# A cross-attention, attention and expert kernel: q Wk^T formed turned, kept in SBUF and dealt by ScalarE and GpSimd; T tiles turned ahead; free expert places kept on chip

## The chip, the cores and the metric

The kernel runs on one core of one Trainium2 chip. The metric is device microseconds of one execution, as the median of several runs. The engines are TensorE (PE; PEld is its weight load), VectorE (DVE), ScalarE (ACT), GpSimd (POOL) and SyncE (SP, which only issues transfers). PSUM holds matmul results; GpSimd does not read it in this kernel.

## The reference

`x` is [8, 64, 512], the context is [8, 1601, 512], all fp32. Three residual steps follow each other.

```
# 1  cross-attention, one head of width 512
q = layernorm(x) @ Wq + bq;  k = ctx @ Wk + bk;  v = ctx @ Wv + bv
x = x + softmax(q @ k.T / sqrt(512)) @ v
# 2  self-attention over the 64 rows of a batch, 16 heads of 32
y = layernorm(x);  n = layernorm(y) * ln_w + ln_b
q, k = l2norm(n @ Wq), l2norm(n @ Wk);  v = y @ Wv
x = x + (sigmoid((q k^T - 0.29514) * 15) * (q.gq) * (k.gk)) @ v @ Wo + bo
# 3  one of 8 experts for each row
z = layernorm(x);  e = argmax(z @ gate_w.T);  zs = z * sigmoid(max logit)
x = x + (zs @ w_up[e].T * silu(zs @ w_gate[e].T)) @ w_down[e].T
```

## The kernel before

The 512 rows of x are four tiles of 128 rows; tile p holds batches 2p and 2p+1, so it is also called pair p. All matrix products are fp32.

**Cross-attention without keys.** Since q k^T = (q Wk^T) ctx^T + q.bk, the kernel never forms k. `project_q` (L278) makes `qpT`, the projected queries turned (columns on partitions). `keyed(p)` (L307) multiplies them by `wkT` into `qk`, 128 queries by 512 columns, with four products of 512 moving columns, and ScalarE copies that to a row tile. `biased` (L314) makes q.bk, which `unturned` (L329) brings into `qb`.

**Context and T tiles.** A pair's context is loaded by `load_group` (L205) in groups: g = 0, 1, 2 are slabs of 128 partitions by four chunks of rows, for each of the two batches (1 MB each), g = 3 is a tail of 65 rows. VectorE turns it in blocks of 32x32: `turn_group` (L230) fills one T tile, which is one quarter q of the 512 columns (four 32-column blocks) for one batch, in four steps, g = 0 to 3. A pair has eight T tiles of 416 keys. They come from a pool `blk` of five buffers; slabs come from a pool of twelve.

**R and the scores.** `scores` (L371) uses row groups: R holds for each 32-column block b the queries of that block, repeated on four groups of 32 partitions a, so that four products of 32 rows run beside each other, each on its own share of keys. For pair 0 R is filled by `spread` (GpSimd repeats the columns) and `fill_queries` (16 TensorE transposes, four ScalarE copies). For the other pairs `turn_queries` (L362) transposes `qk` with four TensorE transposes into PSUM, and `deal_queries` (L366) copies it into R on ScalarE with 16 copies of 32 partitions by 512. R has one buffer: the deals of pair p+1 start after the scores of pair p.

**After the scores.** `softmax` takes maxima on VectorE and four exponentials on ScalarE into `L`. `chances` (L417) transposes a block of `L` and copies it to `pt`; `attend` (L428) multiplies it with the context slabs. `at_turn`, `at_out` finish the tile (`p_po`), then `norm`, `turn`, `unit_q`, `unit_k`, `gates`, `values`, `split`, `align`, `sums`, `back`, `output` are the self-attention of the tile before it, spread between the steps of the pair that is running.

**Experts.** `gate` picks a row's expert (`oh` is its one-hot row). `route` (L733) finds the row's place among the rows of its expert: `pr` sums `ones` x the rows before (`runs`) and `before` x `oh`; `raised` (L773) lifts the count to the next part of 32 between tiles. GpSimd scatters the rows to DRAM (`xd`, `rd`); SP fetches them by part; `up_*`, `over`, `down` are the expert products.

**Order.** TensorE runs in the order of the program text throughout. ScalarE, VectorE and GpSimd do so inside `manual_schedule` blocks; elsewhere a planner orders them by modelled times. `keep_in_program_order` pins a single instruction. Idle transposes (`idle_turns`) stand at TensorE's start.

The main loop of pair p begins each quarter's scores like this, with the T tiles of the next quarter already asked for; the wait for the probabilities stands behind `p_po`:

```
if p == 1:
    keyed(NT - 1)
do((at_out, p - 1))
chance()
turned_qk = turn_queries(p + 1)
```

Of the kernel before, what the change touches and what calls it, by code (L numbers as in the profile page):

```python
# [36 lines left out]
def perceiver_kernel(ctx: ExitStack, tc: tile.TileContext, out: bass.AP, t: dict):  # L37
# [32 lines left out]
    xs = [const.tile([P, D], F32, tag=f"x{i}", name=f"x{i}") for i in range(NT)]  # L70

    def load_x(i):
        nc.sync.dma_start(out=xs[i], in_=t["x"][i * P : (i + 1) * P, :])
# [37 lines left out]
    bk, _ = load_c("xbk", [P, DC], nc.scalar)  # L111
# [93 lines left out]
    def load_group(p, g):  # L205
        got = []
        for b2 in range(2):
            src = t["ctx"][2 * p + b2]
            if g < 3:
                c = slab(f"cx_{p}_{g}_{b2}")  # L210
                rows = src[: 12 * P, :].rearrange("(q c) d -> q c d", c=12)
                nc.sync.dma_start(out=c, in_=rows[:, 4 * g : 4 * g + 4, :])
# [7 lines left out]
    for g in (3, 0, 1, 2):  # L220
        cxs[0, g] = load_group(0, g)
    
# [27 lines left out]

    order = ctx.enter_context(ExitStack())
# [4 lines left out]
    def normal(tiles):  # L256
        stats = []
        for i in tiles:
# [3 lines left out]
            stats.append((mean, rs))  # L262
        xns = []
        for i, (mean, rs) in zip(tiles, stats):
            nc.vector.reciprocal(rs, rs)
            xns.append(row(f"xn{i}"))
            nc.vector.tensor_scalar(xns[-1], xs[i], mean, rs, ALU.subtract, ALU.mult)
# [25 lines left out]
    idle_turns(14)  # L293
    first = {(q, b2): block_tile(0, q, b2) for q, b2 in ((0, 0), (0, 1), (1, 0), (1, 1), (2, 0))}
    with tc.manual_schedule(engines={mybir.EngineType.DVE, mybir.EngineType.Activation}):
        turn_x(0, normal([0])[0])
        project_q(0, 1, [bank(f"qp0_{ec}") for ec in range(DC)])
        later = normal(range(1, NT))
        for g in (3, 0, 1, 2):
            for b2 in range(2):  # L300
                for q in range(3):
                    if (q, b2) in first:
                        turn_group(first[q, b2], 0, q, b2, g)

    qks = {}

    def keyed(p, between=None):  # L307

        cols = slice(p * P, (p + 1) * P)
        ps = projected(qpT[:, :, cols], wkT, f"qk{p}", between)  # L310
        qks[p] = row(f"qk{p}")
        nc.scalar.copy(qks[p], ps)
# [21 lines left out]
    def spread(p):  # L334

        qk = qks.pop(p)
        got = []
        for b0 in range(0, NB, 4):
            q4 = rowp.tile([P, 4, 4, 32], F32, tag="row", name=f"q4_{p}_{b0}")
            nc.gpsimd.tensor_copy(  # L340
                q4,
                qk[:, 32 * b0 : 32 * b0 + 128].rearrange(
                    "p (b d) -> p b d", d=32
                ).unsqueeze(2).to_broadcast([P, 4, 4, 32]),
            )
            got.append(q4)
        return got

# [3 lines left out]

    def fill_queries(p, R, q4s, half):
        for b0 in range(8 * half, 8 * half + 8, 4):
            tp = bank4(f"rt_{p}_{b0}")
            for j in range(4):
                nc.tensor.transpose(
                    tp[:, j, :], q4s[b0 // 4][:, j, :, :].rearrange("p a d -> p (a d)"), ident
                )
            nc.scalar.copy(R[:, b0 : b0 + 4, :], tp)  # L360

    def turn_queries(p):  # L362

        return transposed(qks.pop(p), f"rt_{p}")

    def deal_queries(R, tp, a):  # L366

        for j in range(4):
# [882 lines left out]
```

## Time and profile before

| what | value |
|---|---|
| runs | 290.3, 293.19, 291.98 us; median 291.98 |
| the profiled execution | 290.53 us, of which the span from first to last instruction is 288.8 |
| TensorE busy | 277.4 us, 96% of the span |
| VectorE, ScalarE, GpSimd busy | 158.8, 114.8, 57.7 us |
| scores (L377) on TensorE | 1024 passes |
| T tiles (L232) on VectorE | 96 turns, 62.0 us, 682 ns each |
| R deals (L369) on ScalarE | 48 copies, 27.6 us, 576 ns each |
| moved by DMA | 57.70 MB, mean 200 GB/s |
| granted TensorE clock | 0.998 |

In the rows of a timeline the first number is the start in us from the span's start, the second the duration; then engine, line, operation, output<-inputs, shapes and the count of merged instructions; the bracket gives the idle time of that engine before the row and what ended it. In rows of groups the numbers behind the bar are busy us and mean ns of one. Matmuls are pipelined, so a row's duration is a little longer than the distance to the next row's start. A fp32 matmul of the program shows as two MATMUL rows; a transpose shows as one.

### The profile page before, as it was taken

The page shows a single profiled execution, that of the slowest core. Times are in us where ns is not written, and L with a number is a line of the kernel's source. Part 1 is how long each engine was busy: PE and PEld are TensorE (multiplying, and loading weights), DVE is VectorE, ACT ScalarE, POOL GpSimd, SP SyncE. Part 2 cuts the span into 40 slices and gives each one's busy share as a digit, 9 for nine tenths or more (in the row PEclk, how much of TensorE's full clock was granted, in tenths as well). Part 3 has the DMA queues.
Part 4 walks back from the last instruction along what each step waited for, and adds up shares of the span by engine and source line. Part 5 has one row for each costly group of instructions (what it writes and reads, how often), then busy time and mean ns, then how long its engine had stood idle before and what let it go on. Part 6 is the DMA issues. An engine that isn't in the chain of part 4 may idle for free. (4 is left out here: it accounts for less than half of the span.)

```text
span 288.8 us, 6414 instructions
## 1 busy us (share of the span) xinstructions
PE 277.4 (96%) x2625; PEld 136.8 (47%) x2625; DVE 158.8 (55%) x413; ACT 114.8 (40%) x240; POOL 57.7 (20%) x102
## 2 busy tenths in 40 slices
PE   6999999999999999999999999999999999999991
PEld 4856564436553345555334564443454455343320
DVE  2465487438532776956498694552371476374130
ACT  2232303782057483317769325631426334130110
POOL 5030524000631003100220400022060032413302
PEclk9999999999999999999999999999999999999999
DMA  6999594099799991000499003969990200533401
GB/s 189 350 398 403 188 338 184 3 355 419 268 297 369 406 412 27 5 3 0 161 391 375 22 2 98 341 195 357 376 378 9 75 0 2 161 93 128 168 1 44
DMA packets 20288, 57.70 MB, mean 200 GB/s; under 512 B 2274, under 2 KB 10514, under 8 KB 16544
## 3 DMA queue, kind: packets, MB, share of 16 engines
q1 hardware_dynamic: 17568, 50.37, 48.1%
q0 software_dynamic: 2400, 6.89, 6.7%
q8 instruction: 22, 0.36, 0.5%
q14 instruction: 10, 0.08, 0.1%
q10 hardware_dynamic: 288, 0.00, 0.1%
HBM read 50.94 MB, written 6.84 MB: 200 GB/s over the span
## 5 line engine op out<-in xcount | busy, mean ns | idle before, releaser
L232 DVE STREAM_TRANSPOSE T<-cx 128x512 f32<-128x512 f32 x96 | 62.0, 682 | 23.4 <-DMA cx<-in_ctx_dram 20.4
L377 PE MATMUL sc<-T,R 32*64 32x416 f32 (+2 forms) x1024 | 50.0, 501 | 0.5 <-DVE T L232 0.5
L433 PE MATMUL ac<-cx,pt 128*64 128x512 f32 x192 | 43.8, 598 | 0.0
L377 PEld LDWEIGHTS sc<-T,R 32*64 32x64 f32 x1024 | 26.7, 131 | 17.9 <-issue 5.7
L369 ACT COPY R<-t_rt 32x512 f32<-32x512 f32 x48 | 27.6, 576 | 0.8
L433 PEld LDWEIGHTS ac<-cx,pt 128*64 128x64 f32 x192 | 12.7, 136 | 22.1 <-issue 21.2
L1059 PE MATMUL gu<-wgu,xeT 128*32 128x512 f32 x192 | 22.9, 597 | 0.0
L509 POOL TENSOR_TENSOR gm_k<-qn_k,c_gk 128x512 f32<-128x512 f32 x4 | 5.1, 1271 | 62.7 <-DVE qn_k L504 62.7
L283 PE MATMUL qp<-xnT,w_xWq 128*128 128x128 f32 (+1 forms) x64 | 16.3, 426 | 0.5 <-ACT xnT L274 0.5
L472 POOL TENSOR_TENSOR x<-x,c_bo 128x512 f32<-128x512 f32 x4 | 5.1, 1269 | 55.6 <-DVE xh L471 55.6
L185 PE MATMUL p_q<-w_aWq,xhT 128*128 128x512 f32 x32 | 14.8, 605 | 0.1
L185 PE MATMUL p_qk<-w_xWkT,qpT 128*128 128x512 f32 x32 | 14.6, 598 | 0.1
L185 PE MATMUL p_k<-w_aWk,xhT 128*128 128x512 f32 x32 | 14.7, 596 | 0.0
L388 DVE TENSOR_REDUCE mx<-sc 128x1 f32<-128x416 f32 (+2 forms) x16 | 8.1, 567 | 11.9 <-PE sc L377 11.9
L185 PE MATMUL p_po<-w_xWv,acT 128*128 128x512 f32 x32 | 14.6, 592 | 0.0
L185 PE MATMUL p_o<-w_aWo,cT 128*128 128x512 f32 x32 | 14.5, 596 | 0.0
L185 PE MATMUL p_v<-w_aWv,xvT 128*128 128x512 f32 x32 | 14.4, 592 | 0.0
L283 PEld LDWEIGHTS qp<-xnT,w_xWq 128*128 128x128 f32 x64 | 11.7, 234 | 5.3 <-ACT xnT L274 0.9
L423 ACT COPY pt<-pp 128x512 f32<-128x512 f32 (+1 forms) x16 | 8.1, 505 | 12.8 <-PE pp L421 12.8
L1094 PE MATMUL y<-wd,hT 128*32 128x512 f32 x96 | 11.5, 596 | 0.3 <-ACT hT L1086 0.3
L399 ACT ACT_TABLE_LOAD x3 | 3.8, 1283 | 17.7 <-DVE bias L394 17.7
L1069 DVE TENSOR_TENSOR h<-gu,h 128x256 f32<-128x256 f32 x6 | 2.5, 425 | 14.1 <-ACT h L1068 14.1
(203 smaller groups left out, 377.5 us busy)
## 6 DMA issues: line engine op xcount, KB each, us to landing
cx<-in_ctx_dram SPq DMA_DIRECT2D x24, 1024.0 KB, 10.0
wgu<-in_wgT_dram SPq DMA_DIRECT2D x8, 512.0 KB, 9.2
wgu<-in_wuT_dram SPq DMA_DIRECT2D x8, 512.0 KB
wd<-in_wdT_dram SPq DMA_DIRECT2D x8, 512.0 KB, 7.3
rd<-blank POOLq DMA_DIRECT2D x6, 258.0 KB, 5.5
in<-rd SPq DMA_DIRECT2D x6, 258.0 KB, 3.8
xd<-blank POOLq DMA_DIRECT2D x6, 256.0 KB, 4.8
in<-xd SPq DMA_DIRECT2D x6, 256.0 KB, 7.2
```

The lines of the kernel that those rows point to most:

```text
L185: nc.tensor.matmul(ps, lhsT=srcT[:, dc, :], rhs=w[:, dc, :], start=(dc == 0), stop=(dc == DC - 1),)
L232: nc.vector.transpose(T[:, :, 128 * g : 128 * g + 128].rearrange("p b (c k) -> p b c k", k=32), cxs[p, g][b2][:, :, 128 * q : 128 * q + 12 ...
L283: nc.tensor.matmul(ps[ec][:, : n * P], lhsT=wq[:, dc, ec * P : (ec + 1) * P], rhs=xnT[:, dc, cols], start=(dc == 0), stop=(dc == DC - 1),)
L369: nc.scalar.copy(R[32 * a : 32 * a + 32, j::4, :], tp[32 * j : 32 * j + 32, :, :])
L377: nc.tensor.matmul(sc[a][r : r + S, : WIDTH[a]], lhsT=R[32 * a : 32 * a + 32, b, r : r + S], rhs=Ts[b2][32 * a : 32 * a + 32, j, : WIDTH[a ...
L388: nc.vector.tensor_reduce(mx[:, a : a + 1], sc[a][:, : WIDTH[a]], AX.X, ALU.max)
L423: nc.scalar.copy(pt[:m, :nch, :], tp[:m, :nch, :])
L433: nc.tensor.matmul(ac[r : r + S, :], lhsT=pt[:m, j, r : r + S], rhs=rhs, start=(g == 0 and j == 0), stop=(g == 3),)
L472: nc.gpsimd.tensor_tensor(xs[i], xs[i], bo, ALU.add)
L509: nc.gpsimd.tensor_tensor(heads(gm), heads(qn), gb.unsqueeze(1).to_broadcast([P, H, HD]), ALU.mult)
L1059: nc.tensor.matmul(ps[c, :], lhsT=xTs[k][:, dc, c], rhs=ffw[e][0][:, dc, :], start=(dc == 0), stop=(dc == DC - 1),)
L1094: nc.tensor.matmul(y[c, :], lhsT=hT[:, ic, c], rhs=ffw[e][1][:, ic, :], start=(ic == 0), stop=(ic == IC - 1),)
```

## The change

**q Wk^T turned.** `keyed` now takes `wkT` as the stationary operand and `qpT` as the moving one, so the result comes out with columns on partitions, for one pair (128 moving columns) or for two (256). `keep_keyed` copies it to SBUF (`qkTs`). `turn_queries`, `spread` and `fill_queries` are gone. `deal_queries` reads SBUF, for parts by ScalarE and for parts by GpSimd: for pair 0 two of four partition groups each, for pair 1 all on ScalarE, for pairs 2 and 3 half of each group. A group's deals stand in the turn of the same number.

**Opening.** x becomes one tile, loaded in two transfers; Wq in two instead of four. The tails of pair 0 and `bk` move from the SP and ScalarE queues to GpSimd's, behind a copy that reads the end of Wq. `later = normal(1..3)` stands before `project_q(0)`, and `normal` finishes each tile while the next one's root is taken. There are 15 idle turns and then 2 more. Seven T tiles of pair 0 are asked for at once (two of them in slabs) and turned in the order g = 0, 1, 3, then 2. The first quarter's scores run in two key ranges, 0 to 256 ahead of `biased`, 256 on after group 2 is turned. The whole of pair 0's scores stands inside the manual order.

**Main loop.** Pairs 1 and 2 call `at_out(p - 1, chance)`: the first probability block is transposed between the second and the third product of `p_po`.

**Free places.** `route` makes two products, `before` x `oh` and `ones` x `oh`; VectorE keeps the running counts (`free`) and lifts them to the next part; `raised` and the last product `pc` are gone.

```
-    load_x(0)
+    load_x(0, 1)
     wq = slab("w_xWq")
-    for dc in range(DC):
-        nc.sync.dma_start(out=wq[:, dc, :], in_=t["xWq"][:, dc, :])
-    for i in range(1, NT):
-        load_x(i)
+    for dc in (0, 2):
+        nc.sync.dma_start(out=wq[:, dc : dc + 2, :], in_=t["xWq"][:, dc : dc + 2, :])
+    load_x(1, NT - 1)
...
-    bk, _ = load_c("xbk", [P, DC], nc.scalar)
...
-                nc.sync.dma_start(out=c[: SK - 12 * P, :], in_=src[12 * P :, :])
+                queue = nc.gpsimd if p == 0 else nc.sync
+                ins = queue.dma_start(out=c[: SK - 12 * P, :], in_=src[12 * P :, :])
+                if p < 2:
+                    tc.keep_in_program_order(ins)
...
-    for g in (3, 0, 1, 2):
+    for g in (0, 1, 2):
         cxs[0, g] = load_group(0, g)
...
+    small_loads = tiny(1, "held", "small_loads")
+    tc.keep_in_program_order(nc.gpsimd.tensor_copy(small_loads, wq[:, DC - 1, 0:1]))
+    cxs[0, 3] = load_group(0, 3)
+    bk = load_late("xbk", [P, DC])
...
-    idle_turns(14)
+    idle_turns(15)
     first = {(q, b2): block_tile(0, q, b2) for q, b2 in ((0, 0), (0, 1), (1, 0), (1, 1), (2, 0))}
-    with tc.manual_schedule(engines={mybir.EngineType.DVE, mybir.EngineType.Activation}):
-        turn_x(0, normal([0])[0])
-        project_q(0, 1, [bank(f"qp0_{ec}") for ec in range(DC)])
-        later = normal(range(1, NT))
-        for g in (3, 0, 1, 2):
...
+    for q, b2 in ((2, 1), (3, 0)):
+        T = slabs.tile([P, DC, D], F32, tag="slab", name=f"T_0_{q}_{b2}")
+        first[q, b2] = T[:, :, :416]
...
+    begin = tc.manual_schedule(engines={mybir.EngineType.DVE, mybir.EngineType.Activation})
+    begin.__enter__()
+    turn_x(0, normal([0])[0])
+    later = normal(range(1, NT))
+    idle_turns(2)
+    project_q(0, 1, [bank(f"qp0_{ec}") for ec in range(DC)])
+    for g in (0, 1, 3):
+        turn_first(g)
...
-        ps = projected(qpT[:, :, cols], wkT, f"qk{p}", between)
-        qks[p] = row(f"qk{p}")
-        nc.scalar.copy(qks[p], ps)
...
+        for c in range(DC):
+            if c == DC // 2 and between is not None:
+                between()
+            for ec in range(DC):
+                nc.tensor.matmul(
+                    ps[c * n // DC][:, c % (DC // n), :, :],
+                    lhsT=wkT[:, ec, c * P : (c + 1) * P], rhs=qpT[:, ec, cols],
+                    start=(ec == 0), stop=(ec == DC - 1),
+                )
+        return ps
...
-    def deal_queries(R, tp, a):
...
-        for j in range(4):
-            nc.scalar.copy(R[32 * a : 32 * a + 32, j::4, :], tp[32 * j : 32 * j + 32, :, :])
+    def deal_queries(R, qkT, a, js=range(4), copy=nc.scalar.copy):
...
+        for j in js:
+            copy(R[32 * a : 32 * a + 32, j::4, :], qkT[32 * j : 32 * j + 32, :, :])
...
-        if i > 0:
-            nc.tensor.matmul(pr, lhsT=ones, rhs=runs[-1], start=True, stop=False)
-        nc.tensor.matmul(pr, lhsT=before, rhs=oh[:, i, :], start=(i == 0), stop=True)
...
+        nc.tensor.matmul(ps[:, :E], lhsT=before, rhs=oh[:, i, :], start=True, stop=True)
+        nc.tensor.matmul(ps[:, E : 2 * E], lhsT=ones, rhs=oh[:, i, :], start=True, stop=True)
+        at = tiny(E, "at", f"at{i}")
         if i > 0:
...
+            nc.vector.tensor_tensor(at, ps[:, :E], free[i - 1], ALU.add)
+            nc.vector.tensor_tensor(at, at, oh[:, i, :], ALU.mult)
...
-        for g in range(4):
+        for g in (0, 1, 3, 2):
             cxs[p, g] = load_group(p, g)
...
-    with tc.manual_schedule(engines={mybir.EngineType.Activation}):
-        def turn_later():
-            for i in range(1, NT):
-                turn_x(i, later[i - 1])
...
-        keyed(0, turn_later)
-    q4s = spread(0)
+    R = queries(0)
+    for i in range(1, NT - 1):
+        turn_x(i, later[i - 1])
+    keep_keyed(0, keyed(0, between=lambda: turn_x(NT - 1, later[-1])))
+    for a in range(2):
+        deal_queries(R, qkTs[0], a)
+        deal_queries(R, qkTs[0], 2 + a, copy=nc.gpsimd.tensor_copy)
     project_q(1, NT - 1, [bank(f"qp1_{ec}") for ec in range(DC)])
-    R = queries(0)
-    fill_queries(0, R, q4s, 0)
-    fill_queries(0, R, q4s, 1)
...
+    sc = [bank(f"sc_0_{a}") for a in range(4)]
+    scores(0, 0, R, sc, [first[0, 0], first[0, 1]], hi=256)
     qbT = biased()
...
+    turn_first(2, range(3))
+    turn_first(2, (3,))
+    scores(0, 0, R, sc, [first[0, 0], first[0, 1]], lo=256)
+    first[3, 1] = blocks(0, 3, 1)
+    for q in range(1, 4):
+        scores(0, q, R, sc, [first[q, 0], first[q, 1]])
+        if q == 1:
+            unturned(qbT)
+    begin.__exit__(None, None, None)
...
             if p == 1:
-                keyed(NT - 1)
-            do((at_out, p - 1))
-            chance()
-            turned_qk = turn_queries(p + 1)
+                qk = keyed(NT - 1)
+            at_out(p - 1, chance)
+            if p == 1:
+                keep_keyed(NT - 1, qk)
...
             if 0 < p < NT - 1 and g > 0:
-                deal_queries(R, turned_qk, g - 1)
+                deal_queries(R, qkTs[p + 1], g, range(2))
+                deal_queries(R, qkTs[p + 1], g, range(2, 4), nc.gpsimd.tensor_copy)
...
-    ps = bank("pc")
-    nc.tensor.matmul(ps[:, :E], lhsT=ones, rhs=runs[-1], start=True, stop=True)
```

More of the change, by code (lines that the diff above doesn't have):

```diff
@@ L261, in normal @@
             nc.scalar.activation(rs, var, AF.Sqrt, bias=eps)
[L262 to L267, printed above, removed]
+            if stats:
+                finish(i - 1)
+            stats[i] = mean, rs
+        finish(tiles[-1])
         return xns
@@ L332, in unturned, with scores @@
         nc.vector.tensor_copy(qb, tp[:, 0, ::32])
[L334 to L347, printed above, removed]
     def queries(p):
         return one.tile([P, NB, P], F32, tag="R", name=f"R_{p}")
[L353 to L371 removed]
+    def deal_queries(R, qkT, a, js=range(4), copy=nc.scalar.copy):
+        for j in js:
+            copy(R[32 * a : 32 * a + 32, j::4, :], qkT[32 * j : 32 * j + 32, :, :])
+    def scores(p, q, R, sc, Ts, js=range(4), lo=0, hi=D):
         for j in js:
@@ L694, in tables @@
         )
-    runs = []
+    free = []
     def gate_parts(i):
@@ L963, in perceiver_kernel @@
         if p == 0:
-            for k in range(1, NT):
-                if k < NT - 1:
-                    keyed(k)
-            tables()
+            qk = keyed(1, 2)
         else:
```

108 lines of the change are left out of this document (58 added, 50 removed).

## The prediction

> **What bounds the kernel now.** I read the page first, then the TensorE timeline from the start, then the waits and the timelines of the other engines around each step that moves.
>
> ```profile
> PE 277.4 (96%) x2625; PEld 136.8 (47%) x2625; DVE 158.8 (55%) x413; ACT 114.8 (40%) x240; POOL 57.7 (20%) x102
> ...
> PE   6999999999999999999999999999999999999991
> ```
>
> TensorE is busy 96% of the span of 288.8 us, in every slice but the first and the last. So a part of the change is worth what it takes off TensorE's queue, or what it adds there as waiting. The second view is the TensorE timeline of the opening (start us, duration us, line, tiles, xcount):
>
> ```profile
> 7.19 5.84 PE L283 MATMUL qp<-xnT,w_xWq 128*128 128x128 f32 x32 [0.46 <-ACT xnT L274]
> 13.17 1.95 PE L185 MATMUL p_qk<-w_xWkT,qpT 128*128 128x512 f32 x4
> ...
> 16.42 1.88 PE L185 MATMUL p_qk<-w_xWkT,qpT 128*128 128x512 f32 x4
> 18.14 10.48 PE L283 MATMUL qp<-xnT,w_xWq 128*128 128x384 f32 x32
> 28.46 1.91 PE L357 MATMUL rt<-ident,q 128*128 128x128 f32 x16
> ...
> 32.75 3.02 PE L377 MATMUL sc<-T,R 32*64 32x416 f32 x62 [0.54 <-DVE T L232]
> ```
>
> Each fp32 product is two passes. A pass of 512 columns takes 1.72/4 = 0.43 us (from 16.42 to 18.14), one of 384 takes 10.32/32 = 0.3225 us (18.14 to 28.46): 0.84 ns a column with next to nothing fixed, so 0.11 for 128 columns and 0.22 for 256. A transpose costs 1.84/16 = 0.115. The first projection is slower: asked for by windows, 18 of its 32 passes start between 7.19 and 11.19 (0.21 each), the other 14 take 1.84 us. TensorE's only wait for data here is the 0.54 us before 32.75. The scores of pair 0 end at 45.05. The third view is VectorE's timeline:
>
> ```profile
> 9.41 0.69 DVE L138 BATCH_NORM_STATS2 st_a<-x 128x6 f32<-128x512 f32 x1 [3.85 <-DMA x<-in_x_dram]
> ...
> 31.99 1.30 DVE L232 STREAM_TRANSPOSE T<-cx 128x512 f32<-128x512 f32 x2 [1.68 <-DMA cx<-in_ctx_dram]
> ```
>
> The first context slab of pair 0 is turned at 18.38, the sixth landed just before 31.99, and the first T tile after it (0.65 us) ends TensorE's 0.54 us wait.
>
> **The opening.** Removed there: 16 transposes `rt` (28.46 to 30.30, 1.84 us), the GpSimd `spread` and four ScalarE copies. `keyed(0)` becomes 32 passes of 128 columns, 32 x 0.11 = 3.57 us against 8 x 0.43 = 3.43: +0.14. The three extra idle transposes sit in TensorE's waits before 5.62 (0.35) and 7.19 (0.46) and cost nothing while those stand; without that cover, 3 x 0.23 (3.25/14 of the idle row) = 0.7.
>
> The moved step that matters is `later = normal(...)`: its three square roots now stand on ScalarE ahead of the four `qpT` activations of tile 0, and TensorE's `keyed(0)` is queued behind those. Call L the landing of the one transfer that now holds x1 to x3. From the rows of VectorE (0.69 + 0.18 for a tile's moments, 0.16 + 0.55 for its finish, 0.3 for a root) the third root ends at L + 3.7, `qpT` (1.14) at L + 4.8. Before, x1's moments start at 9.41 and the third tile's at 11.03 without waiting, so all three had landed by 11.03; fewer SP issues (0.46 us each) and half the small ScalarE loads are ahead of it now. I take L = 10.0, with bounds 9.3 and 11.0. Then `keyed(0)` starts at 14.7 instead of 13.17, but with two of the three x transposes behind it; 1.79 + 0.44 + 1.79 later, at 18.7, the 384-column projection starts (18.14 before), and it ends at 29.05.
>
> The first-range scores follow: 64 passes of 256 columns, 3.02 x 256/400 = 1.95, needing only slabs 0 and 1 (landed at 25.9, turned by 28), then `biased` 1.08, to 32.1. Here the second range needs slab 2: landing 31.99 as before, or earlier by up to 2 us because pair 1's tails no longer sit behind it on the same queue; plus 0.65. I take 32.3. The second range (144 columns in the mean, 1.1 to 1.7; I take 1.3), then three quarters (9.09) and `t_qb` (0.33) give 43.1: **-1.9**. With L = 9.3 and an early slab it is 42.1, -2.9; with L = 11.0 and 0.4 more for the split quarter 44.2, -0.8. The other T tiles follow on VectorE 0.65 us apart, ahead of the quarters that read them.
>
> Two more queues are touched. Pair 0's tails and `bk` move to GpSimd, behind a copy that waits for Wq: three issues of 0.53 to 0.75 us, where GpSimd had nothing to do from 4.5 to 18.98. A load from this queue landed 9.2 us after its issue (`c_lnw`), so about 19; the tails are turned at 28, `bk` is read at 31. And two T tiles take the slabs that the two `held` tiles had, so pair 1's second slab pair starts at about 39.5 and 43 instead of 32. A slab took 2.5 us behind another; VectorE asks for it at about 48, and TensorE for the result near 64. Both cost nothing.
>
> GpSimd's part here is eight copies of 32x512 from one set of partitions to another, between 19.4 and about 30. No row has that form. Bounds from the nearest:
>
> ```profile
> L509 POOL TENSOR_TENSOR gm_k<-qn_k,c_gk 128x512 f32<-128x512 f32 x4 | 5.1, 1271 | 62.7 <-DVE qn_k L504 62.7
> ...
> L340 POOL COPY q<-qk 128x512 f32<-128x512 f32 x4 | 2.3, 609 | 14.5 <-ACT qk L312 14.5
> ```
>
> 0.61 us (a copy of as many elements a partition) to 1.27 (two inputs). I take 0.61, the same operation: 4.9 us; at 1.27 it is 10.2, to 29.6, when the last block of the first quarter is just being reached. Hidden at both ends. [...]
>
> [...]
>
> **Later TensorE work.** The 12 transposes `t_rt` go (134.74 to 135.18: 0.44 for four): -1.31. The paired `keyed(1, 2)` is 32 x 0.218 = 6.95 against 6.87, `keyed(3)` as above: +0.08 + 0.14. Routing has 8 small products instead of 10 at 0.22: -0.44; VectorE's extra 8-column adds (0.17) hide behind the 8 us between the last `pr` and the transposes that need its rows.
>
> **A new wait.** In tiles 1 and 2 the first probability block (`pp`) moves from behind `p_po` to its middle.
>
> ```profile
> 126.94 0.66 PE L177 MATMUL t_at<-ident,acs 128*128 128x128 f32 x4
> 127.43 3.60 PE L185 MATMUL p_o<-w_aWo,cT 128*128 128x512 f32 x8
> 130.87 3.60 PE L185 MATMUL p_po<-w_xWv,acT 128*128 128x512 f32 x8
> 134.30 0.60 PE L421 MATMUL pp<-ident,L 128*128 128x128 f32 x4
> 134.74 0.60 PE L177 MATMUL t_rt<-ident,qk 128*128 128x128 f32 x4
> ```
>
> ```profile
> 129.82 1.28 ACT L399 ACT_TABLE_LOAD   x1 [1.54 <-DVE bias L394]
> ...
> 132.85 0.58 ACT L399 ACTIVATE L<-sc,bias 128x384 f32<-128x384 f32 x1
> ```
>
> In tile 2 the scores end at 126.94; `t_at` 0.49, `p_o` 3.44 and half of `p_po` 1.71 bring TensorE to `pp` at 132.58. The fourth exponential ends at 133.43, the one-column one at 133.67: ScalarE loaded its table only after the bias came. TensorE stands 1.05 us, with the second half of `p_po`, the x transposes and all of `attend` queued behind it. If the table is loaded early, the wait is 0. I take 1.05, since this stage's own rows are the nearest. In tile 1 the new `pp` falls at 83.9, after the exponentials' end at 83.66: no wait.
>
> **A wait that shrinks.** ScalarE made 16 deals (0.576 each) per pair; in pairs 2 and 3 it now makes 8, so `sq_k` no longer sits behind four of them (2.37 us from 106.36), nor does the chain over GpSimd's `gm_k` to `kT`, for which TensorE stands 0.58 us before 118.40 and 0.34 before 167.99. VectorE's order may eat part of it: between 0 and -0.92, I take -0.7. GpSimd's deals for pair 3 queue behind the row scatter that ends at 150.1; four at 0.61 end at 152.5, the scores start at 160.65.
>
> **Sum.** -1.9 - 1.31 + 0.22 - 0.44 + 1.05 - 0.7 = **-3.1 us**. The profiled execution took 290.53 (span 288.8), so 287.4; its median of runs is 291.98, 1.45 above it, and I predict **288.9** on that level. All good ends together (-2.9, no wait, -0.92) give -5.4, or 286.6; all bad ends (-0.8, +1.05, 0) -1.3, or 290.7. Runs of one kernel spread about 1 us around their median.
>
> **Rivals.** (1) *The full gain*: the table of tile 2 loads early, the slab lands early: -4.2 to -5.4, about 287.2. For it: pair 1's tails, two transfers of 65 rows, run beside the last slab, and the rate falls there; against it: the table load in the row above stood behind its wait. (2) *The opening gives nothing back*: transfers set the end of pair 0's scores and the x chain comes late: 291.98 - 1.3 to -1.9, about 290.4. For it: six waits of VectorE for slabs, 6.9 us, up to 36 us; against it: the first range now covers what TensorE would wait. (3) *GpSimd's deals become the bound*, and it is slower: place, the first quarter's scores; eight deals of c each have about 11.2 us (19.4 to 30.6) before its last block, so from c = 1.4 us it costs, and from (11.2 + 3.1)/8 = 1.8 the whole gain is gone. At 2.4 us, four times the row, it costs 8: 296.9. Against it: `gs`, a GpSimd copy across partitions, costs 186 ns for 8 elements, the same as a straight one-column copy.
>
> **Chances.** Forecast 0.46, (1) 0.22, (2) 0.22, (3) 0.06, other slower orders 0.04. A measurement of this kernel can tell about 1%, 2.9 us. The forecast's own spread lies a little more than half beyond that, so faster 0.5, within 1% 0.38, slower 0.12 (with part of (2)). The likeliest case alone spans 288.0 to 289.9; the range for 8 in 10 is 285.6 to 291.8.
>
> **What would show it.** Right: no `rt` or `t_rt` rows; scores of pair 0 ending near 43; a TensorE wait of about 1 us on ScalarE's `L` in tile 2; GpSimd deals near 0.6 us; no wait of scores on GpSimd. Wrong: a deal over 1.4 us, `keyed(0)` starting after 16, scores of pair 0 ending after 44.5, or `keyed` passes of 128 columns over 0.13 us, which would add 0.02 x 64 or more.

## The result and the profile after

The changed kernel took 303.53 us in the median of four runs, the kernel before 291.46 on the same chip: a ratio of 1.041, 95% interval 1.036 to 1.047. It is 12 us slower. The forecast was 288.9, in a range up to 291.8. (The 291.98 given ahead of the prediction is the median of three of the four runs of before.)

The profiled execution took 303.54 us, with a span of 301.8 against 288.8. The page of the changed kernel, first TensorE's share and instruction counts, then its busy tenths and its granted clock in 40 slices of the span:

```profile
PE 276.7 (92%) x2724; PEld 142.4 (47%) x2724; DVE 159.6 (53%) x420; ACT 110.1 (36%) x230; POOL 70.8 (23%) x120
...
PE   7699989999999339999899999999999999999991
...
PEclk9989999999999859999999999999999999999997
```

TensorE's busy time is lower than before (276.7 against 277.4), so the work did shrink. But two slices show 3 where before had 9 throughout, and the clock row dips in the same slices, and once near the start. The starts of the same steps in the three timelines of TensorE say where the time went. (The third column is an experiment described below: the blank rows put first.)

| TensorE reaches | before | after | blank rows first |
|---|---|---|---|
| end of pair 0's scores | 44.97 | 46.04 | 46.05 |
| first `p_q` (tile 0) | 100.32 | 110.48 | 102.25 |
| first `al` | 118.40 | 129.36 | 119.57 |
| `t_at` after pair 2's scores | 126.94 | 138.38 | 128.07 |
| pair 2's attention `ac` | 136.14 | 148.20 | 137.89 |
| first `t_xe` (expert rows) | 214.03 | 226.81 | 215.64 |
| end of the span | 288.8 | 301.8 | 290.7 |

Of 13.0 us, 1.07 arise in the opening and 9.1 more by the first `p_q`. Another 0.8 come by the first `al` and 2.0 in all behind it. TensorE's timeline at that place (start, duration, in the bracket the idle time and what ended it):

```profile
99.65 1.08 PE L451 MATMUL ac<-tail,pt 65*64 65x512 f32 x4
110.48 5.26 PE L185 MATMUL p_q<-w_aWq,xhT 128*128 128x512 f32 x8 [9.75 <-DVE xhT L498]
```

TensorE stands 9.75 us for `xhT`, the scaled turned rows of tile 0. Then its `p_q` takes 5.26 us instead of 3.70. The same row of before has no wait:

```profile
100.32 3.70 PE L185 MATMUL p_q<-w_aWq,xhT 128*128 128x512 f32 x8
```

VectorE makes half of `xhT`; its timeline after, and then the two waits for slabs that stood in the same place before:

```profile
100.99 1.30 DVE L237 STREAM_TRANSPOSE T<-cx 128x512 f32<-128x512 f32 x2 [7.00 <-DMA cx<-in_ctx_dram]
...
107.85 0.71 DVE L237 STREAM_TRANSPOSE T<-cx 128x512 f32<-128x512 f32 x1 [5.37 <-DMA rd<-blank]
...
110.06 0.37 DVE L498 TENSOR_SCALAR xhT<-t_xh,c_lnw,c_lnb 128x128 f32<-128x128 f32 x1
```

```profile
93.83 0.71 DVE L232 STREAM_TRANSPOSE T<-cx 128x512 f32<-128x512 f32 x1 [3.56 <-DMA cx<-in_ctx_dram]
...
96.32 1.31 DVE L232 STREAM_TRANSPOSE T<-cx 128x512 f32<-128x512 f32 x2 [1.59 <-DMA cx<-in_ctx_dram]
```

`xhT` is queued on VectorE behind T tiles of pair 2. One of these waited 7.00 us for a context slab, a later one 5.37 us for a transfer `rd<-blank`. That T tile takes one of the five `blk` buffers, the one in which `blank` lies: a zero tile that `blank_rows` (L667) writes twelve times to the expert rows in DRAM. GpSimd's timeline after, and then its memset before, say why this is late:

```profile
79.39 1.91 POOL L385 COPY R<-qkT 32x512 f32<-32x512 f32 x3 [34.05 <-PE sc L395]
81.35 0.52 POOL L669 MEMSET blank<- 128x512 f32 x1
...
82.53 0.56 POOL L672 DMA_DIRECT2D xd<-blank  x1
...
91.03 0.54 POOL L673 DMA_DIRECT2D rd<-blank  x1 [3.69 <-DMA rd<-blank]
93.17 0.54 POOL L672 DMA_DIRECT2D xd<-blank  x1 [1.60 <-DMA xd<-blank]
95.47 0.54 POOL L673 DMA_DIRECT2D rd<-blank  x1 [1.76 <-DMA rd<-blank]
```

```profile
74.78 0.53 POOL L651 MEMSET blank<- 128x512 f32 x1 [28.05 <-PE sc L377]
```

Three deals of pair 2 stand in GpSimd's queue ahead of the `blank` memset. The planner put them there; in the text `blank_rows` comes first. A deal writes R, and R is free only when pair 1's scores end, at 79. So the memset ran at 81.35 instead of 74.78. The twelve transfers then began just as SP started pair 2's slabs (83.70). From issue to landing they took, in the answers for that tile, first after and then before:

```profile
DMA to landing us min/median/max: 2.5/11.5/14.9
```

```profile
DMA to landing us min/median/max: 4.2/5.2/7.7
```

The last one is issued at 95.47, against 82.42 before, as GpSimd waits three times for its own earlier transfers.

In this trace the granted clock falls behind the waits. The same trace by stretches (from:to, length, busy time of TensorE, weight loads, VectorE, ScalarE, GpSimd, then the granted clock, the share of the DMA engines and GB/s):

```profile
7.84:14.66 6.82, 4.37 (x37) 3.97 (x37) 3.94 (x12) 1.55 (x7) 3.05 (x10) 1.00 1.04 403
14.66:18.08 3.42, 3.42 (x18) 3.42 (x17) 1.25 (x3) 1.32 (x4) 0.00 (x0) 0.50 1.02 328
...
103.41:113.65 10.24, 3.17 (x4) 1.51 (x5) 5.80 (x12) 2.62 (x5) 0.00 (x0) 0.50 1.00 418
```

The clock is full from 7.84, half from 14.66 to 18.08, full again, and half for 10.24 us after the long wait began. Before, it was full from 11.42 to 287.9 without a break. (7.84 and 11.42 are the starts of the trace's first clock records. The views count the time ahead of them as full, but TensorE is slow there: four transposes of x take 1.12 us at 5.61, against 0.60 at 18.32.)

The opening, in TensorE's timeline:

```profile
7.18 4.14 PE L299 MATMUL qp<-xnT,w_xWq 128*128 128x128 f32 x32
12.90 0.66 PE L177 MATMUL t_xn<-ident,xn 128*128 128x128 f32 x4 [1.57 <-DVE xn L274]
14.44 0.89 PE L177 MATMUL t_xn<-ident,xn 128*128 128x128 f32 x4 [0.88 <-DVE rs_a L272]
15.12 3.37 PE L343 MATMUL qk<-qpT,w_xWkT 128*128 128x128 f32 x16
...
18.75 1.95 PE L343 MATMUL qk<-qpT,w_xWkT 128*128 128x128 f32 x16
20.54 10.49 PE L299 MATMUL qp<-xnT,w_xWq 128*128 128x384 f32 x32
...
39.24 0.87 PE L395 MATMUL sc<-T,R 32*64 32x385 f32 x7 [1.25 <-issue]
...
46.04 1.13 PE L343 MATMUL qk<-qpT,w_xWkT 128*128 128x256 f32 x4
```

The first projection is faster (4.14 instead of 5.84 us). Then come two waits for x1 and x2 (1.57 and 0.88), the first half of the key products at half clock (3.37 us, the second half 1.95), and near 38 us a wait that ends with "issue", which means that it ends with nothing that the profile shows.

### The profile page after: what moved, and what is told of

It is laid out like the page before. It is cut to its first block, busy times and chain, and to the rows that moved or that the text cites. A ratio compares the mean times of both kernels' runs of the same rounds, so it can differ in the third digit from the quotient of the medians.

```text
span 301.8 us, 6627 instructions
## 1 busy us (share of the span) xinstructions
PE 276.7 (92%) x2724; PEld 142.4 (47%) x2724; DVE 159.6 (53%) x420; ACT 110.1 (36%) x230; POOL 70.8 (23%) x120
## 5 line engine op out<-in xcount | busy, mean ns | idle before, releaser
L395 PE MATMUL sc<-T,R 32*64 32x416 f32 (+5 forms) x1088 | 50.3, 482 | 1.2 <-issue 1.2
L385 POOL COPY R<-qkT 32x512 f32<-32x512 f32 x24 | 14.5, 604 | 56.1 <-PE sc L395 45.6
L185 PE MATMUL p_q<-w_aWq,xhT 128*128 128x512 f32 x32 | 16.4, 659 | 9.8 <-DVE xhT L498 9.8
L385 ACT COPY R<-qkT 32x512 f32<-32x512 f32 x40 | 24.6, 616 | 0.7
L343 PE MATMUL qk<-qpT,w_xWkT 128*128 128x128 f32 (+1 forms) x96 | 16.2, 332 | 0.0
L185 PEld LDWEIGHTS p_q<-w_aWq,xhT 128*128 128x128 f32 x32 | 6.4, 211 | 19.7 <-DVE xhT L498 12.3
L343 PEld LDWEIGHTS qk<-qpT,w_xWkT 128*128 128x128 f32 x96 | 14.9, 213 | 1.4 <-issue 0.7
L185 PE MATMUL p_k<-w_aWk,xhT 128*128 128x512 f32 x32 | 14.7, 596 | 0.0
L299 PE MATMUL qp<-xnT,w_xWq 128*128 128x128 f32 (+1 forms) x64 | 14.6, 388 | 0.0
L503 ACT ACTIVATE xhT<-t_xh,c_lnb,c_lnw 128x128 f32<-128x128 f32 x8 | 3.7, 458 | 25.7 <-DVE xhT L498 25.7
## 6 DMA issues: line engine op xcount, KB each, us to landing
rd<-blank POOLq DMA_DIRECT2D x6, 258.0 KB, 11.5
xd<-blank POOLq DMA_DIRECT2D x6, 256.0 KB, 11.6
```

Of the source, the lines that this page charges most:

```text
L185: nc.tensor.matmul(ps, lhsT=srcT[:, dc, :], rhs=w[:, dc, :], start=(dc == 0), stop=(dc == DC - 1),)
L299: nc.tensor.matmul(ps[ec][:, : n * P], lhsT=wq[:, dc, ec * P : (ec + 1) * P], rhs=xnT[:, dc, cols], start=(dc == 0), stop=(dc == DC - 1),)
L343: nc.tensor.matmul(ps[c * n // DC][:, c % (DC // n), :, :], lhsT=wkT[:, ec, c * P : (c + 1) * P], rhs=qpT[:, ec, cols], start=(ec == 0), s ...
L385: copy(R[32 * a : 32 * a + 32, j::4, :], qkT[32 * j : 32 * j + 32, :, :])
L395: nc.tensor.matmul(sc[a][r : r + S, lo : min(hi, WIDTH[a])], lhsT=R[32 * a : 32 * a + 32, b, r : r + S], rhs=Ts[b2][32 * a : 32 * a + 32, ...
```

## The experiments

The ratio is always to the kernel before, run beside each on the same chip, with its 95% interval. "Theory A" for the large loss is the chain just read: deals ahead of the blank rows, late writes that collide with the slabs, a buffer that stays taken, and `xhT` behind T tiles.

**Blank rows first.** The GpSimd deals of pair 2 are pinned behind what the text has in front of them. Only GpSimd's order differs.

```
+    behind = {
+        1: lambda to, of: tc.keep_in_program_order(nc.gpsimd.tensor_copy(to, of)),
+        2: nc.gpsimd.tensor_copy,
+    }
...
-                deal_queries(R, qkTs[p + 1], g, range(2, 4), nc.gpsimd.tensor_copy)
+                deal_queries(R, qkTs[p + 1], g, range(2, 4), behind[p])
```

> The kernel after, with GpSimd's eight query deals for pair 2 pinned behind the two memsets and twelve transfers of the blank rows; every other engine's order is as in after. Theory A (late blanks: the deals wait for scores(1) to end, so the blank rows are written 6.6 us later, run into pair 2's context loads and keep VectorE's next T tile waiting for their buffer): the blank transfers are issued from about 75 us as before, the 9.75 us wait of p_q for xhT falls below 1 us, the cold clock behind it goes too, and the time is 303.5 - 11 = 291.5 to 292.8. Rival B (pair 2's context is late because of its own order, tails ahead of the third slab, or because of what moved to the two slabs): p_q still waits 5 us or more, time 299 or more.

291.94 us, ratio 1.002 (0.997 to 1.007): the time is that of the kernel before again. The memset ran at 75.6, and the transfers landed as fast as before. The answers for the `blank` tile and for TensorE's waits:

```profile
L669 POOL MEMSET blank<- x1: 524/524/524, 75.6 to 75.6; 128x512 f32 x1
...
DMA to landing us min/median/max: 3.2/5.4/6.8
```

```profile
PE p_q L185 <- DVE xhT L498: 1.5, 1, 1.5
```

In this execution 1.5 us of the wait stay. SP starts pair 2's slabs 0.95 us later here than before (83.69 against 82.74), but the wait isn't the same in every run: it is 0.34 us in "the first probability block behind the projection" below, which is this kernel up to that point.

**The deals on ScalarE.** The 16 deals of pairs 2 and 3 that GpSimd made go back to ScalarE; nothing is pinned.

```
-                deal_queries(R, qkTs[p + 1], g, range(2, 4), nc.gpsimd.tensor_copy)
+                deal_queries(R, qkTs[p + 1], g, range(2, 4))
...
-                deal_queries(R, qkTs[p + 1], 0, range(2, 4), nc.gpsimd.tensor_copy)
+                deal_queries(R, qkTs[p + 1], 0, range(2, 4))
```

> The kernel after, with all sixteen deals of pairs 2 and 3 on ScalarE (before's engine), none on GpSimd. Theory A: the blank rows run early again, so 303.5 - 11 plus what eight more ScalarE copies of 0.62 us a pair give back of the al wait (at most 0.9): 291.5 to 293.5. Rival B: 299 or more, as nothing but the deals changes engine. Rival C (the cost is the deals' own slowness on GpSimd, not the blanks behind them): as A in time, but then pinning the blanks ahead of the deals must not help.

293.26 us, ratio 1.006 (1.001 to 1.011). It agrees with theory A. With the run before, it rules out that the deals' own time on GpSimd was the cost: with the deals on GpSimd, but behind the blanks, the time is no worse.

**The blank tile in a buffer of its own kind.** The blanks stay late, but hold a row buffer.

```
-        blank = blkp.tile([P, D + 4], F32, tag="blk", name="blank")
+        blank = rowp.tile([P, D + 4], F32, tag="row", name="blank")
```

> The kernel after, with the blank tile taken from the row buffers instead of the five that T tiles and L share; the blanks stay late (behind all eight deals). It parts the two ways in which late blanks could cost: T's wait for the buffer, 5.37 us in after, and the late landing of pair 2's context, 7.00 us of wait in after against 3.56 + 1.59 before. If both count, 297 to 300; if only the buffer counts, 292 to 294; if only the transfers count, 302 to 304.

297.08 us, ratio 1.016 (1.007 to 1.026): both ways count, about half each (the memset ran at 84.3 here, 3 us later than in after, so the halves are rough). VectorE's timeline and TensorE's:

```profile
100.32 1.30 DVE L237 STREAM_TRANSPOSE T<-cx 128x512 f32<-128x512 f32 x2 [6.78 <-DMA cx<-in_ctx_dram]
...
101.74 0.67 DVE L237 STREAM_TRANSPOSE T<-cx 128x512 f32<-128x512 f32 x1
```

```profile
104.93 6.41 PE L185 MATMUL p_q<-w_aWq,xhT 128*128 128x512 f32 x8 [4.52 <-DVE xhT L498]
```

The wait for `blank` is gone; the one for the slab is still 6.78 us. TensorE stands 4.52 instead of 9.75 us, and `p_q` still runs mostly at half clock (6.41 us; the clock is half from 103.60 to 110.43).

**The kernel before with late blanks.** Only this is added to the kernel before: GpSimd copies a column of the exponentials of pair 1 ahead of the memset, which so waits.

```
+        tc.keep_in_program_order(
+            nc.gpsimd.tensor_copy(tiny(1, "held", "held_blank"), L[:, 0, 96:97])
+        )
-        nc.gpsimd.memset(blank[:, :D], 0.0)
+        tc.keep_in_program_order(nc.gpsimd.memset(blank[:, :D], 0.0))
```

> The kernel before, with one thing added: GpSimd copies one column of pair 1's last exponential (L, key columns of group 3) ahead of the blank memset, which so starts at about 82 instead of 74.8. Nothing of the change is in it. Theory A: it falls into the same wait: p_q or the T tiles stand 8 to 11 us near 100 us, time 300 to 303.5. Rival B (late blanks matter only together with the changed order of T tiles and slabs): 291 to 294.

304.51 us, ratio 1.044 (1.037 to 1.051). The memset ran at 83.3, and nothing of the change is needed for the loss. TensorE's timeline:

```profile
98.77 1.08 PE L433 MATMUL ac<-tail,pt 65*64 65x512 f32 x4
111.15 1.22 PE L185 MATMUL p_q<-w_aWq,xhT 128*128 128x512 f32 x1 [11.30 <-DVE xhT L480]
```

**`xhT` without VectorE.** In the kernel after, ScalarE makes all four parts of tile 0's `xhT`.

```
-            if dc % 2 == 0:
+            if dc % 2 == 0 and i > 0:
                 nc.vector.tensor_scalar(
```

> The kernel after with one edit: tile 0's xhT, four copies with scale and bias, is made by ScalarE alone, none of it by VectorE; blank rows, deals, buffers and loads stay as in after. Theory A (TensorE stands 9.75 us only because two of these copies are queued on VectorE behind T tiles that wait for the late slab and for the blank tile's buffer): the blanks and the T tiles stay late (VectorE's waits of 5 to 7 us near 94 to 108 remain), but p_q starts near 101 instead of 110.5, its clock stays up, and the time is 292 to 296. Rival B (the next reader of the late T tiles, pair 2's scores, or the norms behind them on VectorE, simply take over the wait): TensorE stands 6 us or more at a later place, time 299 or more.

300.52 us, ratio 1.032 (1.025 to 1.039): rival B, mostly. `p_q` starts on time, at 101.68 behind the attention that ends there. But pair 2's scores, which read the late T tiles, then wait instead:

```profile
101.68 3.70 PE L185 MATMUL p_q<-w_aWq,xhT 128*128 128x512 f32 x8
...
115.34 1.14 PE L395 MATMUL sc<-T,R 32*64 32x416 f32 x2 [3.09 <-DVE T L237]
118.41 5.10 PE L395 MATMUL sc<-T,R 32*64 32x416 f32 x62 [1.93 <-DVE T L237]
```

5.0 us of waiting and 62 passes at half clock (5.10 us instead of 3.02 for 64) take the place of 9.75 us. The first attention also starts 1.0 us later than in after (55.37), with the clock of the opening at half up to 20.26 here. So moving `xhT` gives back 3 to 4 of the 11.6 us; the late T tiles, wherever they are met, cost the rest.

**The opening: fill the waits.** From here on every kernel made from the changed one has the blank rows first. Here idle transposes stand in the two waits for x.

```
+    idle_turns(13)
     for i in range(1, NT - 1):
         turn_x(i, later[i - 1])
+        if i == 1:
+            idle_turns(8)
```

> The kernel with the blank rows first, plus idle transposes in TensorE's two waits of the opening (13 ahead of the second x tile's transposes, 8 behind them), so that it doesn't stand still from 11.4 to 12.8 and from 13.5 to 14.4. Theory A (those waits make the throttle halve the clock, granted 0.5 from 14.76 to 18.17, which doubles the first half of the key products): the granted clock stays 1.0 from about 8 us, the first 16 passes take 1.8 to 2.0 us instead of 3.5, and the scores of pair 0 end 1.4 to 1.7 earlier than 46.05, near 44.5. Rival B (transposes don't hold the clock, or what follows is bound by VectorE's T tiles): the clock falls as before, or the scores still end at 45.5 or later. In total time at most 1.7 us less than blank_first: near the bound of what can be told.

292.95 us, ratio 1.010 (1.005 to 1.016): no gain. The clock part of theory A holds, its end does not. TensorE's timeline and two stretches of the clock:

```profile
13.92 1.95 PE L343 MATMUL qk<-qpT,w_xWkT 128*128 128x128 f32 x16
...
17.93 10.49 PE L299 MATMUL qp<-xnT,w_xWq 128*128 128x384 f32 x32
...
31.27 3.40 PE L395 MATMUL sc<-T,R 32*64 32x160 f32 x100
36.58 2.74 PE L395 MATMUL sc<-T,R 32*64 32x416 f32 x28 [1.91 <-issue]
```

```profile
6.20:36.90 30.70, 28.54 (x339) 21.53 (x345) 20.67 (x44) 12.20 (x26) 11.80 (x26) 1.00 0.92 354
36.92:40.34 3.42, 3.42 (x37) 1.20 (x29) 0.16 (x1) 0.00 (x0) 2.44 (x2) 0.50 0.30 89
```

The key products run at full clock (1.95), and the 384-column projection starts at 17.93 instead of 20.46. But the issue wait grows to 1.91 us, and the clock falls right behind it, for 3.4 us. The scores end at 45.71, so 0.34 of 2.5 us is left. Later `p_q` waits 1.25 us, and the clock is half for 3.4 us behind that wait (101.78 to 105.19), so that `p_q` takes 5.2 us to the next row instead of 3.5. In this execution that is more than the 0.34 us gained; the totals of the two kernels agree within their intervals.

**The opening: the order of before.** Tile 0's projection stands ahead of the moments of tiles 1 to 3 again, and the three x transposes stand between the two halves of the key products (that part of the edit is left out below).

```
     turn_x(0, normal([0])[0])
-    later = normal(range(1, NT))
     idle_turns(2)
     project_q(0, 1, [bank(f"qp0_{ec}") for ec in range(DC)])
+    later = normal(range(1, NT))
...
```

> The kernel with the blank rows first, plus the order of before in the opening: tile 0's projection and its four ScalarE copies ahead of the moments and roots of tiles 1 to 3, and the three x transposes between the two halves of the key products. Theory A (waiting for x1 to x3 costs the opening its gain, by the wait itself and the clock): TensorE's waits at 11.4 to 14.4 shrink below 1 us in all, the 384-column projection starts near 17 instead of 20.46, and the scores of pair 0 end near 43.7 (then bound by the T tiles of the third slab, about 31.4), 2.4 us earlier. Rival B (T tiles and the 1.3 us stall set the end whatever the start): the scores end at 45.5 or later.

289.48 us, ratio 0.997 (0.994 to 1.001). The 384-column projection starts at 18.89, 1.6 us earlier. The scores still end at 45.99. Again a 1.25 us issue wait (to 37.59), and a clock at half from 38.36 to 41.77. The start of the projection moved 1.57 us and the end of the scores 0.06: the stretch from the issue wait to the end takes 8.40 us (37.59 to 45.99) against 6.81 with blank rows first (39.24 to 46.05), where the clock stayed full. So what was gained in front was lost to the half clock right behind this wait.

**The opening: one key range.**

```
-    scores(0, 0, R, sc, [first[0, 0], first[0, 1]], hi=256)
     qbT = biased()
...
-    scores(0, 0, R, sc, [first[0, 0], first[0, 1]], lo=256)
+    scores(0, 0, R, sc, [first[0, 0], first[0, 1]])
```

> The kernel with the blank rows first, with the first quarter's scores of pair 0 made in one key range of up to 416 columns behind the bias product, not in two: 64 passes fewer. Theory A (the 1.3 us in which TensorE waits for nothing but issue before 39.24 comes from the short passes, which use up instructions faster than they are fetched: an instruction fetch runs from 36.75 to 37.73): the stall goes and the scores of pair 0 end near 44.5 instead of 46.05. Rival B (the stall has another cause): it stays over 1 us, and the scores end at 45.7 or later, as the first range then covers nothing.

287.61 us, ratio 0.990 (0.987 to 0.993). TensorE's timeline:

```profile
30.60 1.16 PE L363 MATMUL qb<-qpT,c_xbk 128*32 128x128 f32 x32
31.69 5.82 PE L395 MATMUL sc<-T,R 32*64 32x416 f32 x128
...
43.44 3.94 PE L343 MATMUL qk<-qpT,w_xWkT 128*128 128x256 f32 x17
```

The issue wait is gone, and the scores end at 43.44, 2.6 us earlier. They start at 31.69 without a wait, so by then the third slab's T tiles of quarter 0 are there, and the first range had nothing to cover here.

**Two ranges in the kernel before.** Is the split bad in itself?

```
-                scores(p, q, R, sc, Ts)
+                if p == 0 and q == 0:
+                    scores(p, q, R, sc, Ts, hi=256)
+                    scores(p, q, R, sc, Ts, lo=256)
+                else:
+                    scores(p, q, R, sc, Ts)
```

> The kernel before, with one edit: the first quarter's scores of pair 0 in two key ranges, one behind the other, 64 passes more. Theory A (the short passes use up instructions faster than they come): a wait of TensorE for nothing but issue, 1 to 2 us, between 33 and 40 us, and the scores of pair 0 end at 45.5 to 47, against 45.05. Rival B (the stall in the changed kernel belongs to its order of loads and GpSimd issues there): no such wait, scores end at 44.5 to 45.2, since the first range doesn't wait for the third slab's T tiles (0.54 us before).

289.88 us, ratio 0.995 (0.992 to 0.999): not so. Theory A's wait is there, but is 0.39 us:

```profile
34.30 3.70 PE L377 MATMUL sc<-T,R 32*64 32x416 f32 x67
38.39 5.80 PE L377 MATMUL sc<-T,R 32*64 32x416 f32 x125 [0.39 <-issue]
```

It says more of the wait, though. If I count TensorE's records (products, weight loads and its own waits) from the start of each trace, the issue wait stands behind record 705 in every kernel that has one: in this one, and in the eight others with two ranges (after, and the experiments made from it without the one-range edit). "Fill" has 21 more transposes in front and stops 21 passes earlier (100 instead of 121 passes of its row). Each time the trace has one transfer of 16384 bytes on the instruction queue just around it (36.74 to 37.71 in after), and TensorE goes on 1.3 to 1.5 us after it ended (at 39.24 in after). With one range the 705th record starts at 39.85, 2.3 us after that transfer ended, and nothing waits. The one reading that I found to fit them all is that TensorE runs out of instructions: short passes (0.03 us each, two records) use them up before this transfer brings more. No trace names what TensorE waits for, so this stays an estimate. The times agree with it: in all fifteen kernels, before among them, this transfer starts 2.6 to 4.0 us after record 449 (33.46 and 36.74 in after, 35.97 and 39.29 in before). The nine that stall need 3.9 to 4.8 us from there to record 705 without the wait (4.02 in after), the six that do not 5.9 to 6.1 (6.06 in before). What sets the start of the transfer is not shown.

**The first probability block behind the projection.** For pair 2 only.

```
-            at_out(p - 1, chance)
...
+            else:
+                at_out(p - 1)
+                chance()
```

> The kernel with the blank rows first, with the first probability block of tile 2 behind the whole output projection, as before, not in its middle. Theory A (it waits for ScalarE's exponential there, 0.83 us): TensorE's wait for L falls below 0.2 us and pair 2's attention starts 0.6 to 0.9 earlier counted from the end of its scores. Rival B: the wait turns up elsewhere, no gain. In total time too small to be told.

288.57 us, ratio 0.997 (0.994 to 1.000). No wait for `L` is left:

```profile
130.67 3.60 PE L185 MATMUL p_po<-w_xWv,acT 128*128 128x512 f32 x8
134.11 0.60 PE L439 MATMUL pp<-ident,L 128*128 128x128 f32 x4
```

From `t_at` to pair 2's attention it takes 8.77 us (126.74 to 135.51) against 9.82: 1.05 us.

**Three repairs.** Blank rows stand first, there is one key range, and `pp` stands behind the projection.

> The kernel after with three repairs at once: the blank rows first, the first quarter's scores in one key range, tile 2's first probability block behind its output projection. If the three costs are separate, they add: 11.6 us (blanks), 2.6 (two ranges, measured as the end of pair 0's scores, 46.05 to 43.44) and 1.05 (the wait for L, measured from the end of pair 2's scores to its attention, 9.82 to 8.77); so about 3.5 us less than the blanks-first kernel, ratio to before 0.984 to 0.990, scores of pair 0 ending at 43.4, no wait for L over 0.2. Rival: gains in front are given back at a later wait (the fetch of the experts' rows, xd, or p_q): ratio 0.992 or more.

286.92 us, ratio 0.986 (0.981 to 0.991), within the 0.984 to 0.990 expected if the gains add. In the profiled execution Wq landed later (a wait of 0.45 before the second half of the first projection), x too, and the scores ended at 44.44.

**Repairs, filled waits, third slab in another order.** VectorE turns the third slab for quarter 0 ahead of the other quarters' tails.

```
-    for g in (0, 1, 3):
+    for g in (0, 1):
         turn_first(g)
+    turn_first(3, (0,))
...
-    turn_first(2, range(3))
-    turn_first(2, (3,))
+    for q in range(4):
+        turn_first(2, (q,))
+        if q < 3:
+            turn_first(3, (q + 1,))
```

> The three repairs plus the idle transposes in the opening's two waits and, on VectorE, the third slab's T tiles of quarter 0 ahead of the tails of the other quarters. Theory A (with the stall of the short passes gone, the clock and the T tiles of the third slab set the opening): the granted clock stays 1.0 from about 7 us, the scores of pair 0 start near 29.5 and end at 41.3 to 42.3, 1 to 2 us less than the three repairs alone; ratio 0.978 to 0.986. Rival B (the third slab lands after 30): the scores start at 31 or later and end at 43 or later, no gain.

287.23 us, ratio 0.986 (0.982 to 0.989). The opening did as theory A said: scores from 29.79 to 42.33. The total gained nothing. The profiled execution was the longest of six (290.82 us, the others 285.61 to 288.06), and in it the time was given back at `p_q`:

```profile
98.96 6.75 PE L185 MATMUL p_q<-w_aWq,xhT 128*128 128x512 f32 x8 [1.96 <-DVE xhT L499]
```

A wait of 1.96 us, and then half clock for 6.8 us. TensorE waits for `xhT`, which VectorE makes in part behind pair 2's T tiles. This shows what makes that one execution long; what took the gain of the opening in the other five is not shown.

**The same, with tile 0's `xhT` on ScalarE.**

> The kernel with the three repairs, the filled waits and the third slab's order, plus tile 0's xhT on ScalarE alone. There p_q stood 2.0 us for xhT behind VectorE's T tiles, and the clock fell to half for 6.8 us behind it (p_q took 6.58 instead of 3.54). If that was the queue: no wait of p_q over 0.5, granted clock 1.0 throughout, 3 to 5 us less, ratio to before 0.968 to 0.977. Rival: the wait turns up at pair 2's scores, ratio 0.983 or more.

286.35 us, ratio 0.983 (0.978 to 0.988), from 285.66 to 287.25 in six runs: the best of the study, 5 us under before. `p_q` does not wait (96.96), the granted clock is 1.0 from 4.78 to 281.25, and no wait turned up at the scores. The step from the run before is within its interval, and its ratio is the one that the rival named (0.983 or more), though no wait turned up. So the loss profiled at `p_q` in the run before was hardly in every execution there.

## Why the prediction was wrong

The failed step is the one on GpSimd, which ends in "Hidden at both ends" and enters the sum as nothing. It weighed the eight deals of pair 0 by their own time, and for these it held: the scores start at 30.96 without a wait. For pair 2 it looked at no queue at all; for pair 3 at what stands ahead of the deals. What stands behind pair 2's deals, the blank rows, it never named, nor that a deal waits for R and so for the end of pair 1's scores. The runs showed in its place that the blank rows run 6.6 us late behind these deals, that their transfers collide with the slabs (11.5 us to landing in the median, 5.2 before) and keep a `blk` buffer, and that TensorE stands 9.75 us for `xhT`. That is worth 11.6 us (303.5 to 291.9).

- *Duration of a deal.* It was taken as 0.61 us. The page of after has:

```profile
L385 POOL COPY R<-qkT 32x512 f32<-32x512 f32 x24 | 14.5, 604 | 56.1 <-PE sc L395 45.6
...
L385 ACT COPY R<-qkT 32x512 f32<-32x512 f32 x40 | 24.6, 616 | 0.7
```

  The duration was right. Rival (3) put its price on it; the loss came at 0.604 us, by order alone.
- *"Both cost nothing"* (tails and `bk` on GpSimd's queue, T tiles in two slabs): no wait on them shows in TensorE's waits. The text looked at the pool of slabs only and did not ask which tile follows `blank` in the five `blk` buffers.
- *Opening, -1.9.* It measured +1.07, and the scores ended past 44.5, the sign that the text had set for being wrong. The landing of x was near enough (10.5, taken 10.0), and `keyed(0)` started at 15.12, against 14.7. Two terms were missing. First, its first half was priced at 0.11 a pass (1.79 us) and took 3.20 to the next row, as the clock was at half; the 384-column projection so started at 20.54, not 18.7. Second, from the second range to the end of the scores 10.7 us were counted and 12.2 measured: the issue wait (1.25) and what stands around it. The split, taken as pure cover, was the part that cost: with one range the scores end 2.6 us earlier.
- *Idle transposes.* The sum has no gain for them. The first projection got 1.70 us shorter (5.84 to 4.14), with the full clock from 7.84 instead of 11.42. In two runs the clock record is full while TensorE had done nothing but transposes: from 4.89 with the deals on ScalarE and from 4.78 in the last run, where the first projection starts at 6.82 and 6.79 (the four transposes ahead of it take 0.66 us, not 1.12). In "fill", with 21 more of them, it was full from 6.20 to 36.90. The gain is not certain either: in "the order of before", with the same 17 transposes, the first clock record starts only at 11.05, and the projection took 5.56 us. The key products then waited for x anyway (1.57 and 0.88 us in after).
- *The new wait, +1.05.* It measured 0.83 in the bracket, and 1.05 when the block was put back. That was right.
- *The wait that shrinks, -0.7.* From `p_q` to `al`, with blank rows first, 18.08 became 17.32 and 17.84 became 17.32: -1.28, more than the bound of -0.92.
- *Transposes and key products, -1.31 + 0.22.* From `t_at` to the attention of pair 1 -0.29 (-0.30 by the sum), in pair 2 with the block put back -0.43 (-0.44). That was right.
- *Routing, -0.44.* It was not seen: from pair 2's attention to `t_xe` 77.89 became 77.75, of which -0.52 is the wait above and +0.24 a new wait for the fetched rows. That leaves about +0.1.

## What to carry to other kernels

When work moves to another engine's queue, the first question is not how long it takes, but what it waits for and what is then queued behind it; here 0.6 us copies held up transfers that nobody waits for, until these ran into a busier time and kept a shared buffer. A gain in front of a wait is often kept only if the next input is early too: look for what the engine meets next, its data and its clock, and, if the reading of the issue wait is right, its instructions. Splitting a product into short passes can cost more than its columns: here TensorE stood 1.25 us behind them in the changed kernel, and 0.39 in the kernel before, whose total did not suffer.

## What the runs showed of the hardware

- TensorE stood with nothing to wait for that the profile shows, 0.4 to 1.9 us behind the same record in nine kernels, wherever two key ranges were used. It went on 5.7 to 6.3 us after it passed record 449 (5.78 in after). That it waited for instructions is my reading. The transfers of 16384 bytes on the instruction queue speak for it: in after 22 of them start between 20.32 and 295.16, with 5316 of TensorE's records from the first to the last, one transfer for 253; in before 21 start between 20.78 and 282.74, with 5153 records, one for 258.
- The stretches at half clock lasted 3.42 us (14.66 to 18.08), 3.41 (38.36 to 41.77 in the order of before), 6.83 (98.29 to 105.12 with the repairs and filled waits) and 10.24 (103.41 to 113.65). The clock fell behind waits of 2.45 us in sum in the opening, 1.91 in "fill", 1.25 in the order of before. Yet 1.53 us before `p_q` with blank rows first did not lower it, nor did 1.77 and 0.88 in the opening with the deals on ScalarE. What decides between these was not tried.
- Writes of 256 KB from GpSimd's queue landed in 5.4 us (median) when most were issued ahead of the 1 MB slab loads, and in 11.5 beside these; GpSimd then stood 3.69, 1.60 and 1.76 us before it issued the next ones.
